# Dilation beside attention: half of a row's re-reading moved to the other of its two pieces

## The chip, the cores and the metric

The kernel runs on one core of a Trainium2 chip. The metric is the device time of one execution in microseconds (us), lower is better; the time of a kernel is the median of several executions.

## The reference

Sixteen graphs of 1024 nodes with 128 features pass through an attention layer and a graph layer of three rounds. What matters here is that both layers need the adjacency `adj` (16 x 1024 x 1024, f32): the attention masks and weights its scores with it, and the graph layer uses a *dilated* adjacency, from which entries were removed row by row in a fixed order, each removal seen by later rows:

```
# layer 0: attention over existing edges, weighted by adj
scores = einsum('bhnd,bhmd->bhnm', q, k) / sqrt(16)
scores = where(adj == 0, -inf, scores)
attn   = softmax(scores) * adj ;  attn /= attn.sum(-1) + 1e-8
# the pattern that layer 1 uses: n runs over the 1024 rows in order
row  = carry[n];  num = row.sum()
sf   = where(num > 10, (num + 1) // 2, 1)
rm   = row & (cumsum(row) % sf == 0)      # if num > 1 and the node is not masked
carry[n] = row & ~rm;  carry[:, n] &= ~rm # the column of the same node too
# layer 1: three rounds of  adj_dilated @ h / deg @ Wr + h @ Wx + b, normalised
```

## The kernel before, in words

**Attention.** For each graph `b`, column half `c` and 128-row block `m` of keys there is one turn (256 turns), and each turn has two *steps*, for `g` = 0 and 1, so that there are 512 steps. A step is: sixteen small matmuls that put minus infinity where there is no edge (line 554) and four score matmuls (560) on PE; two exponentials of 128x1024 on ACT (598); two products with the adjacency of 128x1024 on VectorE, DVE (603); and, one step later, eight value matmuls and eight sums on PE (487, 492). At `g` = 0 a turn also turns a block of `adj` over for the turn after next: load (188), transposes (505), ACT's copy and edge test (508, 512), the store of the turned block (509) and six small DMAs that copy the edge test to other partitions (516, 517; tile `nomask`). All DMAs named here are issued by SP, one after the other.

**Dilation.** It runs as a generator beside the attention, in eight blocks of 128 rows of all sixteen graphs (`k` = 0 to 7). In a block the removals inside the diagonal square are found by rounds of counting, and then each graph's row block is finished ("a row" below means one graph's 128 rows of the block, so a block has sixteen). The generator yields its cost and where its next piece may go; `beside_attention` (951) spends pieces at an even pace over the 512 steps, and a piece marked "A" comes only behind a step of `g` = 0, one marked "B" behind a step of `g` = 1, "1" behind either. PE, ACT and DVE run their instructions in the order in which they are written down; SP's DMAs are put in order by the framework's own scheduler.

**A row's two pieces** (the loop at 896, counter `i`, three rows in flight):
- the "A" piece: a running sum along row `i` on DVE (900, tile `both`), eight transposes of row `i - 2` on PE (907) and ACT's copy of them (909, tile `et`);
- the "B" piece: two absolute values for row `i` on ACT (915, `wr`); for row `i - 1` on DVE the removals (924, 928, 930, tile `er`); the fetch of an earlier block's removals for row `i + 1` (893, `gm`); and for row `b = i - 2` the re-reading for the next block: `read` takes the signs of the freshly loaded rows `ad` in two parts, the columns up to and with the next diagonal square (699) and the rest (703), each with a count; then on DVE the merge of row and column (937), the stores of the removals (938, 940, 942; `mr_d`), `survive` for row `b - 2` (716: takes the removed entries out of the signs, with a count), `fetch_removed` for `b` (710, tile `gl`) and the load of `ad` for row `i` (683).

The tiles `ad`, `gl`, `gm` and `et` have two buffers each. The last two calls of `survive` of a block, for rows 14 and 15, are made by `last_two` (721) between the first parts of the next block: one behind the product 749 and 750, one behind the first scan (756). The sixteenth row's `gl` is fetched from what the sixteenth row's `et` has just stored.

Of the kernel before, what the change touches and what calls it, by code (L numbers as in the profile page):

```python
# [15 lines left out]
AF = mybir.ActivationFunctionType  # L16
# [18 lines left out]
def swept(ctx: ExitStack, tc: tile.TileContext, t: dict, out: bass.AP, flag: bass.AP):  # L35
# [8 lines left out]
    nc = tc.nc  # L44
    x, adj, nodemask = t["x"], t["adj"], t["nodemask"]
    B, N, D = x.shape
# [120 lines left out]
    def first_part(p1):  # L167
# [90 lines left out]
        signs = one.tile([P, NB, 2, B], F32, name="signs")  # L258
# [200 lines left out]
        def fetch_first(b, queue):  # L459

            first_rows[b] = shared.tile([P, N], F32, name=f"ad_0_{b}", tag="mr", bufs=4)
            queue.dma_start(first_rows[b], adj[b, :P, :])
# [188 lines left out]
        def dilation():  # L651
# [9 lines left out]
            def rk(b, lo, hi):  # L661
                return rks[b // (B // 2)][:, b % (B // 2), lo:hi]

            blocks = {}
# [10 lines left out]
            def fetch(k, b):  # L675

                if k == 0:
                    if b not in first_rows:
                        fetch_first(b, nc.gpsimd)
                    blocks[0][2][b] = first_rows.pop(b)  # L680
                    return
                ad = shared.tile([P, N], F32, name=f"ad_{k}_{b}", tag="ad", bufs=2)
                nc.sync.dma_start(ad, adj[b, k * P : (k + 1) * P, :])
                blocks[k][2][b] = ad

            def read(k, b):
                ad = blocks[k][2].pop(b)
                n1 = (k + 1) * P
                if k == 0 and b % 2:
                    for part, of, count in (  # L690
                        (rk(b, 2, 2 + n1), ad[:, :n1], signs[:, k, 0, b : b + 1]),
                        (rk(b, 2 + n1, N + 2), ad[:, n1:], blocks[k][1][:, b : b + 1]),
                    ):
                        nc.vector.scalar_tensor_tensor(
                            part, of, 0.0, nothing.to_broadcast([P, of.shape[-1]]), ALU.add, ALU.not_equal,
                            accum_out=count,
                        )
                    return
                nc.scalar.activation(
                    rk(b, 2, 2 + n1), ad[:, :n1], AF.Sign, accum_out=signs[:, k, 0, b : b + 1]  # L700
                )
                if n1 < N:
                    nc.scalar.activation(
                        rk(b, 2 + n1, N + 2), ad[:, n1:], AF.Sign, accum_out=blocks[k][1][:, b : b + 1]
                    )

            def fetch_removed(k, b):
                if k > 0:
                    gl = shared.tile([P, N], BF, name=f"gl_{k}_{b}", tag="gl", bufs=2)
                    nc.sync.dma_start(gl[:, : k * P], mr_d[b][:, k, : k * P])  # L710
                    blocks[k][3][b] = gl

            def survive(k, b):
                if k > 0:
                    part = rk(b, 2, 2 + k * P)
                    nc.vector.scalar_tensor_tensor(
                        part, part, 0.0, blocks[k][3].pop(b)[:, : k * P], ALU.add, ALU.is_gt,
                        accum_out=blocks[k][0][:, b : b + 1],
                    )

            def last_two(k):
                for b in (B - 2, B - 1):
                    survive(k, b)
                    yield
# [11 lines left out]
            for k in range(NB):  # L736
                n0 = k * P
                n1 = n0 + P
# [62 lines left out]
                parts = small.tile([P, 2, B], F32, name=f"parts_{k}", tag="parts", bufs=2)  # L801
# [82 lines left out]
                more = k + 1 < NB  # L884
# [4 lines left out]
                def known(b):  # L889

                    if k > 0 and b < B:
                        gms[b] = shared.tile([P, N], BF, name=f"gm_{k}_{b}", tag="gm", bufs=2)
                        nc.sync.dma_start(gms[b][:, :n0], mr_d[b][:, k, :n0])

                known(0)
                for i in range(B + 2):
                    b = i
                    if b < B:
                        row = rk(b, 0, N + 2)
                        nc.vector.tensor_tensor_scan(  # L900
                            pair_sums[b % 2], row[:, 0::2], row[:, 1::2], 0.0, ALU.add, ALU.add
                        )
                    b = i - 2
                    if 0 <= b:
                        pe = ps_d.tile([P, NB, P], BF, name=f"pe_{k}_{b}", tag="d")
                        for j in range(NB):
                            nc.tensor.transpose(pe[:, j, :], ers[b][:, j * P : (j + 1) * P], ident_bf)
                        ets[b] = pool.tile([P, NB, P], BF, name=f"et_{k}_{b}", tag="et", bufs=2)
                        nc.scalar.copy(ets[b], pe)
                    yield (1.3 if i < B else 0.0), "B"  # L910
                    b = i
                    if b < B:
                        wrs[b] = pool.tile([P, N], F16, name=f"wr_{k}_{b}", tag="wr", bufs=2)
                        for t, at in enumerate((at_even, at_odd)):
                            nc.scalar.activation(  # L915
                                wrs[b][:, t * HN : (t + 1) * HN], pair_sums[b % 2][:, t : t + HN], AF.Abs,
                                bias=at[:, b : b + 1], scale=2.0,
                            )
                    b = i - 1
                    if 0 <= b < B:  # L920
                        er = ers[b] = pool.tile([P, N], BF, name=f"er_{k}_{b}", tag="er", bufs=3)
                        wr = wrs.pop(b)
                        for t in range(2):
                            nc.vector.tensor_scalar(
                                er[:, t::2], wr[:, t * HN : (t + 1) * HN], off[:, b : b + 1], allof[:, b : b + 1],
                                ALU.is_equal, ALU.max,
                            )
                        nc.vector.tensor_tensor(er, er, rk(b, 2, N + 2), ALU.mult)
                        if k > 0:
                            nc.vector.tensor_tensor(er[:, :n0], er[:, :n0], gms.pop(b)[:, :n0], ALU.max)  # L930
                    known(i + 1)
                    b = i - 2
                    if 0 <= b:
                        if more:
                            read(k + 1, b)
                        er, et = ers.pop(b), ets.pop(b)
                        nc.vector.tensor_tensor(er[:, n0:n1], er[:, n0:n1], et[:, k, :], ALU.max)
                        nc.sync.dma_start(mr_d[b][:, k, :n1], er[:, :n1])
                        if k > 0:
                            nc.sync.dma_start(mr_d[b][:, :k, n0:n1], et[:, :k, :])  # L940
                        if more:
                            nc.sync.dma_start(mr_d[b][:, k + 1 :, n0:n1], et[:, k + 1 :, :])
                            if b >= 2:
                                survive(k + 1, b - 2)
                            fetch_removed(k + 1, b)
                    if more and i < B:
                        fetch(k + 1, i)
                    yield (2.9 if i < B else 1.2), ("A" if i < B + 1 else 1)
                late = last_two(k + 1) if more else iter(())

        def beside_attention():
# [102 lines left out]
    def output_part(L, b, c, hT, prev, tag):  # L1054

        py = bank(f"py_{L}_{b}_{c}", tag).rearrange("p (k d) -> p k d", d=D)
        for i in range(HB):
            n = (c * HB + i) * P
            nc.tensor.matmul(py[:, i, :], hT[:, n : n + P], wts[f"Wl{L}"], start=True, stop=True)
        yield  # L1060
        k0 = c * HB
        for i in range(HB):
            k = k0 + i
            nc.vector.scalar_tensor_tensor(
                prev[:, k, :], py[:, i, :], mf2[:, b * NB + k : b * NB + k + 1], prev[:, k, :],
                ALU.mult, ALU.add,
            )
        if c == 1:
            nc.gpsimd.dma_start(acc_d[L][b], prev)
# [142 lines left out]
    with tc.manual_schedule(  # L1212
# [6 lines left out]
        for L in range(3):  # L1219
# [10 lines left out]
            for b in range(B):  # L1230
                more = b + 1 < B
# [3 lines left out]
                for c in range(2):  # L1235
                    i = (L * B + b) * 2 + c
# [10 lines left out]
                    parts = []  # L1247
                    if c == 1 and L > 0:
                        at_end = b + 2 >= B
                        parts = [output_part(L - 1, b, h, hT, prev, held.pop(0) if at_end else "y") for h in range(2)]  # L1250
# [727 lines left out]
```

## Time and profile before

| | |
|---|---|
| three runs | 3395.78, 3398.22 and 3401.01 us, median 3398.22 |
| the profiled execution | 3396.91 us, of which the span from the first to the last instruction is 3395.1 |
| granted TensorE clock | 0.995 |
| the attention's exponentials | first at 20.1 us, last step at 2318.0: 4.50 us a step |
| of it, one row of a block (two steps) | 9.2 us in blocks 0 to 3, 9.7 in block 6, 8.9 in block 7 |
| signs, first part (699), 128x256 to 128x1024 | 425 ns to 1054 ns |
| signs, second part (703), 128x768 to 128x128 | 848 ns to 308 ns |
| `survive` (716), 128x128 to 128x896 | 284 ns to 1083 ns, and 82 ns to read its count |
| `gl` (710), issue to landing | 1.6 to 6.2 us, median 3.6 |
| `nomask` (516, 517), issue to landing | median 2.7 us |

A step is timed from the start of its first exponential to that of the next step's. Engines: PE is TensorE, DVE VectorE, ACT ScalarE, POOL GpSimd, SP the engine that issues DMAs. A group of instructions is read as: line, engine, operation, output<-inputs, shape, count | busy us, mean ns of one | idle time of the engine just before them and what ended it. The profiled execution is one run; sums below are made against its own time.

### The profile page before, as it was taken

How to read it: one execution, taken by the hardware profiler on the slowest of the kernel's cores; microseconds unless marked ns; L12 is line 12 of the kernel's file. 1: busy time of each engine (PE TensorE's matmuls, PEld its weight loads, DVE VectorE, ACT ScalarE, POOL GpSimd, SP SyncE). 2: the span in 40 equal slices, each digit the busy share in tenths (PEclk: the TensorE clock that was granted, in tenths of full speed). 3: DMA queues.
4: the chain of work that ended last, by engine and by line, in shares of the span. 5: the costliest groups of instructions: out<-in, count | busy, mean ns of one | idle time of the engine just before them, and what ended most of it. 6: DMA issues, size and time to landing. Idle time of an engine off the chain costs nothing. (4 is left out here: it accounts for less than half of the span.)

```text
span 3395.1 us, 86338 instructions
## 1 busy us (share of the span) xinstructions
PE 3310.6 (98%) x34855; PEld 1872.4 (55%) x34855; DVE 3025.5 (89%) x5399; ACT 2305.4 (68%) x3909; POOL 164.2 (5%) x253
## 2 busy tenths in 40 slices
PE   8999999999999999999999999999999899999997
PEld 3333333333333333333334334336999899999997
DVE  7898989989989998998998999897888899988887
ACT  7699689779879969968976986884232344423334
POOL 2000000000000000000000000000000000000000
PEclk9999999999999999999999999999999999999999
DMA  7357456547637736845863773677999799989996
GB/s 242 108 168 206 137 149 199 161 129 221 188 122 213 221 122 183 238 144 158 236 190 122 237 240 119 189 228 261 346 341 343 284 353 350 353 323 350 352 351 222
DMA packets 650123, 772.28 MB, mean 227 GB/s; under 512 B 173264, under 2 KB 569168, under 8 KB 637424
## 3 DMA queue, kind: packets, MB, share of 16 engines
q1 hardware_dynamic: 632672, 708.58, 64.4%
q0 software_dynamic: 15456, 57.30, 5.0%
q8 instruction: 275, 4.51, 0.6%
q14 instruction: 136, 1.11, 0.1%
q10 hardware_dynamic: 1584, 0.79, 0.1%
HBM read 508.50 MB, written 157.29 MB: 196 GB/s over the span
## 5 line engine op out<-in xcount | busy, mean ns | idle before, releaser
L603 DVE TENSOR_TENSOR w<-e,aT 128x1024 f32<-128x1024 f32 x1024 | 1205.5, 1219 | 138.4 <-ACT e L598 136.8
L598 ACT ACTIVATE e<-sc 128x1024 f32<-128x1024 f32 x1024 | 991.9, 1022 | 333.6 <-PE sc L560 332.6
L1132 PE MATMUL pg<-y,aT 128*128 128x128 f32 (+1 forms) x6144 | 729.8, 275 | 0.0
L1132 PEld LDWEIGHTS pg<-y,aT 128*128 128x128 f32 x6144 | 707.9, 192 | 0.0
L487 PE MATMUL acc<-w,both 128*32 128x512 f32 x4096 | 586.7, 605 | 3.1 <-DVE w L603 2.6
L560 PE MATMUL sc<-qT,kT 32*128 32x512 f32 x4096 | 584.4, 640 | 0.3 <-ACT qT L315 0.3
L492 PE MATMUL acc<-e,eps 128*32 128x512 f32 x4096 | 573.1, 592 | 0.0
L146 DVE SCALAR_TENSOR_TENSOR aT<-mr,aT 128x1024 f32<-128x1024 bf16 x384 | 458.8, 1217 | 0.0
L492 PEld LDWEIGHTS acc<-e,eps 128*32 128x32 f32 x4096 | 150.6, 110 | 294.6 <-issue 289.6
L1155 ACT ACTIVATE sq<-o 128x512 f32<-128x512 f32 x96 | 60.6, 631 | 328.5 <-DVE o L1150 328.5
L554 PEld LDWEIGHTS <-never 32*32 32x32 bf16 x8192 | 80.9, 88 | 347.9 <-issue 325.6
L554 PE MATMUL sc<-nomask,never 32*32 32x512 bf16 x8192 | 252.3, 385 | 16.8 <-ACT e L598 12.3
L1173 ACT COPY hT<-pt 128x512 f32<-128x512 f32 x96 | 56.3, 586 | 289.3 <-PE pt L1169 280.0
L560 PEld LDWEIGHTS sc<-qT,kT 32*128 32x128 f32 x4096 | 160.1, 183 | 116.9 <-issue 116.1
L505 PEld LDWEIGHTS pa<-ident,a 128*128 128x128 f32 x1024 | 107.7, 141 | 181.4 <-issue 129.7
L487 PEld LDWEIGHTS acc<-w,both 128*32 128x32 f32 x4096 | 92.8, 108 | 156.2 <-issue 65.4
L915 ACT ACTIVATE wr<-both,th 128x512 f16<-128x512 f16 x256 | 172.1, 730 | 7.1 <-DVE both L900 6.9
L505 PE MATMUL pa<-ident,a 128*128 128x128 f32 x1024 | 168.3, 287 | 6.4 <-DMA a<-in_adj 5.7
L512 ACT ACTIVATE nomask<-aT 128x512 bf16<-128x512 f32 x256 | 161.4, 630 | 8.1
L1150 DVE SCALAR_TENSOR_TENSOR o<-pg,rdeg,mine 128x128 f32<-128x128 f32 x384 | 108.1, 344 | 55.9 <-PE pg L1132 52.6
L508 ACT COPY aT<-pa 128x512 f32<-128x512 f32 x256 | 152.7, 597 | 5.3 <-PE pa L505 4.3
L900 DVE TENSOR_TENSOR_SCAN both<-rk 128x513 f16<-128x513 bf16 x128 | 155.9, 1218 | 0.0
(228 smaller groups left out, 3894.9 us busy)
## 6 DMA issues: line engine op xcount, KB each, us to landing
aT<-aT_d SPq DMA_DIRECT2D x94, 2048.0 KB, 9.9
mr<-mr_d SPq DMA_DIRECT2D x188, 512.0 KB, 6.0
aT_d<-aT SPq DMA_DIRECT2D x256, 256.0 KB, 4.0
a<-in_adj SPq DMA_DIRECT2D x253, 256.0 KB, 3.7
ad<-in_adj SPq DMA_DIRECT2D x112, 512.0 KB, 4.2
nomask<-nomask SPq DMA_DIRECT2D x512, 96.0 KB, 2.7
nomask<-nomask SPq DMA_DIRECT2D x512, 64.0 KB, 2.7
nomask<-nomask SPq DMA_DIRECT2D x512, 32.0 KB, 2.7
```

Source lines behind the costliest of these rows:

```text
L146: nc.vector.scalar_tensor_tensor(part, mrs[h][:, j : j + 2, :].rearrange("p j n -> p (j n)"), 0.0, part, ALU.is_equal, ALU.mult)
L487: nc.tensor.matmul(acc[g][32 * j : 32 * j + 32, :], v1[:, m, (2 * j + g) * HW : (2 * j + g) * HW + 32], ws[j // 2][:, j % 2, :], start=(m ...
L492: nc.tensor.matmul(acc[g][32 * j : 32 * j + 32, :], eps8, es[j // 2][:, j % 2, :], start=False, stop=(m == NB - 1),)
L505: nc.tensor.transpose(pa[:, k * P : (k + 1) * P], a[:, k, :], ident)
L512: nc.scalar.activation(nomask[:, 0, :], aT[:, 0, :], AF.Relu, bias=1.0, scale=-1e38, accum_out=zeros[:, i : i + 1])
L554: nc.tensor.matmul(scs[j // 2][to : to + 32, j % 2, :], never[rows, rows], nomask[rows, j, :], start=True, stop=False, tile_position=(32 * ...
L560: nc.tensor.matmul(scs[j // 2][:, j % 2, :], kT[rows, mm], qTs[c][rows, g, :], start=False, stop=True, tile_position=(32 * j, 0),)
L598: nc.scalar.activation(e, scs[q], AF.Exp, scale=1.0 / math.sqrt(HD))
L603: nc.vector.tensor_tensor(w, es[q], aT.to_broadcast([P, 2, HN]), ALU.mult)
L900: nc.vector.tensor_tensor_scan(pair_sums[b % 2], row[:, 0::2], row[:, 1::2], 0.0, ALU.add, ALU.add)
L915: nc.scalar.activation(wrs[b][:, t * HN : (t + 1) * HN], pair_sums[b % 2][:, t : t + HN], AF.Abs, bias=at[:, b : b + 1], scale=2.0,)
L1132: nc.tensor.matmul(pg[:, i // 2, at : at + width], aT[:, j, i * P : (i + 1) * P], y[:, j, :width], start=(j == 0), stop=(j == NB - 1),)
```

## The change

In each row's piece, the second part of the signs (703), `survive`, `fetch_removed` and the load of the next `ad` leave the "B" piece and are put at the front of the "A" piece that follows it, half a row later; for row 15 they come in the first piece of the next block. The costs that pieces are given change so that each row's sum stays as it was (1.3 + 2.9 becomes 2.1 + 2.1). No instruction is added or taken away.

```diff
-            def read(k, b):
-                ad = blocks[k][2].pop(b)
+            def read(k, b, parts=(0, 1)):
+                ad = blocks[k][2][b] if parts == (0,) else blocks[k][2].pop(b)
...
-                nc.scalar.activation(
-                    rk(b, 2, 2 + n1), ad[:, :n1], AF.Sign, accum_out=signs[:, k, 0, b : b + 1]
-                )
-                if n1 < N:
+                if 0 in parts:
+                    nc.scalar.activation(
+                        rk(b, 2, 2 + n1), ad[:, :n1], AF.Sign, accum_out=signs[:, k, 0, b : b + 1]
+                    )
+                if 1 in parts and n1 < N:
...
+                def other_half(b):
+                    if more and b >= 0:
+                        read(k + 1, b, (1,))
+                        if b >= 2:
+                            survive(k + 1, b - 2)
+                        fetch_removed(k + 1, b)
+                    if more and 0 <= b + 2 < B:
+                        fetch(k + 1, b + 2)
+
                 known(0)
                 for i in range(B + 2):
+                    other_half(i - 3)
...
-                    yield (1.3 if i < B else 0.0), "B"
+                    yield (2.1 if i < B else 0.8), "B"
...
-                            read(k + 1, b)
+                            read(k + 1, b, (0,))
...
-                            if b >= 2:
-                                survive(k + 1, b - 2)
-                            fetch_removed(k + 1, b)
-                    if more and i < B:
-                        fetch(k + 1, i)
-                    yield (2.9 if i < B else 1.2), ("A" if i < B + 1 else 1)
+                    yield (2.1 if i < B else 0.4), ("A" if i < B + 1 else 1)
+                other_half(B - 1)
                 late = last_two(k + 1) if more else iter(())
```

The program that results has every other piece at the same step as before. On SP, in block 4's last row as an example, the order before was: `et` stores, `er` store (938), `gl`, `ad`, `a` (188), `aT_d` (509), six `nomask`. After it is: `et` stores, `ad`, `er` store, `a`, `aT_d`, six `nomask`, `gl`, `ad`. It is the same in blocks 0, 1, 2, 5 and 6 (without the `ad` loads in block 6); in block 3 `gl` stands right behind `a`.

## The prediction

> **What bounds the kernel now.** I read the page's busy shares first, then busy time in thirteen rows (i = 3 to 15) of each block, then SP's waits, then the timeline where one block ends and the next begins.
>
> ```profile
> span 3395.1 us, 86338 instructions
> ...
> PE 3310.6 (98%) x34855; PEld 1872.4 (55%) x34855; DVE 3025.5 (89%) x5399; ACT 2305.4 (68%) x3909; POOL 164.2 (5%) x253
> ...
> L716 DVE SCALAR_TENSOR_TENSOR rk<-rk,gl 128x768 bf16<-128x768 bf16 x16 | 15.2, 952 | 1.2 <-DMA gl<-mr_d 1.2
> ```
>
> No engine is the bound by its share alone; ACT's 68% is an average over unlike stages. The last line is to be kept in mind: of 112 calls of `survive`, DVE waits for a `gl` 1.2 us before one of the sixteen in block 5 (0.8 and 0.3 in blocks 1 and 3). The windows below are the rows of blocks 0, 2, 4, 5, 6 and 7: length; busy PE, weight loads, DVE, ACT, POOL; clock; DMA.
>
> ```profile
> 196.80:316.30 119.50, 116.60 (x1266) 43.30 (x1262) 106.52 (x171) 118.74 (x210) 2.81 (x3) 1.00 0.69 198
> ...
> 751.30:870.90 119.60, 116.04 (x1263) 43.65 (x1259) 114.25 (x185) 118.36 (x209) 3.88 (x6) 1.00 0.74 214
> ...
> 1306.20:1427.80 121.60, 117.59 (x1260) 44.43 (x1259) 119.15 (x198) 119.59 (x211) 5.00 (x6) 1.00 0.79 235
> 1587.50:1711.00 123.50, 118.69 (x1253) 45.17 (x1246) 120.10 (x196) 119.92 (x212) 5.00 (x6) 1.00 0.81 239
> 1872.40:1998.80 126.40, 120.89 (x1260) 44.53 (x1263) 123.38 (x197) 119.99 (x188) 4.97 (x6) 1.00 0.81 244
> 2157.90:2273.40 115.50, 112.96 (x1250) 41.14 (x1251) 110.00 (x156) 102.62 (x149) 6.60 (x10) 1.00 0.75 226
> ```
>
> Inside the rows ACT is busy 99% of the time in blocks 0 to 3; DVE draws level in block 4 and passes it in 5 and 6. Block 7, without signs, runs shorter. Cut at each step's start, ACT works 4.1 us in "A" and 5.1 in "B"; DVE, cut at its own line 603, 3.8 in "A" and 4.45 (block 0) to 5.75 (block 6) in "B". The halves are uneven, but their buffers join them: in blocks 0 to 3 ACT stands idle only about 0.1 us a row.
>
> Where a block ends, the picture is another. Timeline, last row of block 4:
>
> ```profile
> 1450.15 0.47 SPq L938 DMA_DIRECT2D mr_d<-er  x1
> ...
> 1451.64 0.33 SPq L710 DMA_DIRECT2D gl<-mr_d  x1
> 1452.07 0.38 SPq L683 DMA_DIRECT2D ad<-in_adj  x1
> 1452.54 0.38 SPq L188 DMA_DIRECT2D a<-in_adj  x1
> 1452.93 2.28 DVE L756 TENSOR_TENSOR_SCAN w<-go_on,up 128x1024 f16<-128x1024 bf16 x1
> ...
> 1455.13 0.80 DVE L716 SCALAR_TENSOR_TENSOR rk<-rk,gl 128x640 bf16<-128x640 bf16 x1
> ...
> 1455.86 2.35 DVE L603 TENSOR_TENSOR w<-e,aT 128x1024 f32<-128x1024 f32 x2
> ...
> 1457.70 0.59 SPq L517 DMA_DIRECT2D nomask<-nomask  x1
> ```
>
> `gl` of row 15 leaves SP at 1451.64 and lands at 1454.42; the last `survive` reads it at 1455.13, with attention's products right behind it on DVE. So 0.7 us are to spare. From 1445.2 to 1472.4 DVE is busy 26.14 of 27.2 us, ACT 18.55: here DVE leads.
>
> **The change part by part.**
>
> *Second signs, "B" to "A".* ACT's sum per row is unchanged. The part costs 848 ns (block 0, for block 1's row), 741, 634, 527, 418, 308 and nothing (block 6): ACT becomes about 4.95/4.25 in block 0, 4.5/4.8 in block 5, unchanged in block 6. Its price is bounded above by nothing removed, and below by all idle time being recovered: window less the busier of ACT and DVE, over blocks 0 to 6, is 0.8 + 0.9 + 1.2 + 1.5 + 2.0 + 3.4 + 3.0 = 12.8 us (blocks 1 and 3 read the same way). A loss would need ACT to wait for scores; they are made 1.5 us after an exponential ends, and at least 2 us of other ACT work stays between exponentials in either half.
>
> *survive, "B" to "A", 0.28 to 1.08 us and 0.08 for its count.* DVE becomes 4.1/4.1 in block 0 and 4.9/4.7 in block 6. Queued behind it in "A" are the running sum and then "B"'s products. ACT's 915 waits for that sum, 1.56 us after it in block 0 and 0.58 in block 6 on average. But in "B" the same instruction no longer stands before the "A" products, which now start 0.11 (block 0) to 1.72 us (block 6) after their exponentials: what is put in front of the sum is mostly given back there. I price both moves inside the rows together at -4 us of the possible 12.8, nearer to nothing because blocks 0 to 3 have no idle time to give, and keep -12.8 and +5 (0.05 us a row in 112 rows, half the ACT idle seen) as ends.
>
> *The new costs* of the pieces shift nothing: every other piece keeps its step. *The load of `ad`* comes half a row later; it is read about 14 us later at a landing of 4.2 (median). Hidden; uncovered it would cost ACT at most that 4.2 a row.
>
> *fetch_removed.* Inside the rows a `gl` has some 10 us between landing and its `survive`, and both move by half a row: nothing. It also gains: before, SP stood waiting for the store of `et` to land:
>
> ```profile
> SPq L710 <- DMA mr_d<-et: 70.4, 66, 3.4
> ```
>
> That wait is 1.1 us each of 66 times and goes, as eight other DMAs are now in between. At a block's end, though, the two readers in `last_two` do not move: `survive` of row 15 still stands behind the first scan, while `gl` of row 15 is now issued behind `a`, `aT_d` and the six `nomask` (the order on SP in the section on the change). Those take 5.3 us on SP in block 0 (338.83 to 344.14) and 5.75 in block 4 (1452.54 to 1458.29). Counted from the `er` store's issue: before, `gl` follows after 1.5 to 1.9 us; after, after 0.5 + 0.9 + the six `nomask` (3.75 to 4.8). From the difference I take 0.6 (row 14's landing wait, 1.1, is gone earlier; an `ad` of 0.5 has come in; 1.1 in block 6, which has no such `ad`).
>
> | block | `gl` landed | later by | `survive` started | DVE late by |
> |---|---|---|---|---|
> | 0 | 341.87 | 3.45 | 342.51 | 2.8 |
> | 1 | 620.88 | 2.6 | 620.90 | 2.6 |
> | 2 | 897.9 (issue + 3.1, the median of the others) | 2.85 | 898.90 | 1.9 |
> | 3 | `gl` stands behind `a` alone | 0 | 1176.87 | 0 |
> | 4 | 1454.42 | 4.0 | 1455.13 | 3.3 |
> | 5 | 1740.08 | 4.1 | 1740.10 | 4.1 |
> | 6 | 2025.05 | 2.5 | 2026.05 | 1.5 |
>
> The sum is 16.2 us. Who waits behind it: DVE's products of the next step, PE's value matmuls of them, then scores and exponentials. How much passes through? In block 4 the value matmuls begin at 1458.40, 1.3 us after the first product is done; but DVE runs on without a gap to 1470, and at 1463.3 and 1468.5 PE is already waiting for it (0.32 and 0.72 us). A late DVE therefore stays late: I take all 16. The lower bound takes off that 1.3 at six ends, leaving 8; the upper one adds row 14's `gl`, which moves too (in blocks 1, 3 and 5 by my count 2 us past its reader), and is 24.
>
> *Order of `nomask`.* It comes about 1.5 us earlier at a block's end. Once this helps: in block 1 PE's mask matmuls at 616.64 wait for a `nomask`. -1 us.
>
> [...]
>
> **The sum**: -4 - 1 + 16 = +11 us on the profiled execution's 3396.9 (3395.1 of span and 1.8 around it): 3408. That execution lay 1.3 below the runs' median, so I forecast 3409 against 3398.2.
>
> **The rivals.**
>
> *Balance wins, faster.* If `gl` of row 15 lands in time after all (its place on SP matters only if SP is behind; it decides when SP reaches the last `nomask` less than 1 us after the old issue of `gl`), only the moves in the rows count: -5 to -13, about 3390. For it: DVE and ACT both stand idle 0.2 to 0.5 us a row in blocks 5 and 6. Against: SP issued the store of row 15's `er` 4.5 to 8.0 us after DVE had it ready (937), in all seven blocks, so SP is behind. Chance 0.13.
>
> *The late DVE is absorbed, no change.* Inside the rows a product is ready 0.9 to 2.1 us before its matmul; if that spring is there at the ends too, 8 us pass, 4 come back and 1: +3, 3401. Against it stand the two PE waits above. Chance 0.22.
>
> *SP chokes in the rows too, slower still.* `gl` now waits for a `survive` of the same piece, and everything on SP behind it, the next `nomask` too, waits as well. `nomask` lands 3 to 6 us before its matmuls on average; if that is used up, 0.2 us a row in 112 rows, 22 more: 3430. Against: SP gets to `gl` some 7 us into the piece, DVE to `survive` at 4. Chance 0.08.
>
> **How the numbers follow.** The forecast has 0.57, with its own range 3402 to 3418. A difference under 0.2% (6.8 us) can't be told from none here, so slower begins at 3405.0 and faster ends at 3391.4. Slower: 0.08, and 0.52 of the forecast's 0.57: 0.60. Same: 0.22 and 0.05 of the forecast, 0.27. Faster: 0.13. The range, 3393 to 3424, leaves out most of the fast case and the choke.
>
> **What would show it.** Right: six idle times of DVE before 716, ended by `gl`, of 1.5 to 4 us, none in block 3; the steps at a block's end longer by as much; windows inside the rows shorter by up to 0.3 us a row in blocks 5 and 6; ACT's busy time unchanged. Wrong: `gl` landing before its `survive` everywhere; or those waits there and the next block's first removals no later; or rows longer, with PE waiting for `nomask`.

## The result, and the profile after

| | before | after |
|---|---|---|
| median | 3396.41 us (3393.52 to 3401.01, 6 runs) | 3427.61 us (3419.55 to 3432.16, 6 runs) |
| ratio to before | | 1.0087, 95% interval 1.0072 to 1.0102 |
| profiled execution, its span | 3396.91, 3395.1 us | 3428.24, 3426.4 us |
| attention's last step begins at | 2318.0 us | 2346.9 us |

The change made the kernel 31 us slower; 11 were forecast, with 3424 as the upper end. 28.9 of the 31.3 us between the two spans are lost inside attention, and 2.4 behind it, where executions of the same code differ by as much (see "What stays open"). Cut at the steps of the exponentials, they lie so (a row of a block is two steps; lines of the changed kernel behind 698 are 1 to 11 higher than before: `survive` is 717, the fetch of `gl` 711, the first signs 700, the second 704):

| part, all blocks together | after less before, us |
|---|---|
| rows 0 to 2 | -3.4 |
| rows 3 to 15 | +4.2 |
| block ends: the ten steps behind the rows, blocks 0 to 6 | +29.5: 0.8, 2.8, 4.7, 1.0, 6.1, 7.1, 7.0 |
| ahead of the rows of block 0 | -1.2 |
| the rest between the blocks | -0.2 |

The first line is no gain: one second reading of signs (848 ns in block 0 to 308 in block 5) has left that stretch for the block's end, where the same time comes back. So the ends lose about 26 and the rows 4.

The page of after, its span and the busy time of each engine:

```profile
span 3426.4 us, 86274 instructions
...
PE 3317.4 (97%) x34855; PEld 1864.2 (54%) x34855; DVE 3026.4 (88%) x5399; ACT 2304.6 (67%) x3909; POOL 161.5 (5%) x253
```

The busy time of DVE and ACT is the same as before to 1 us: to these two nothing was added but waiting. PE's grew by 6.8 us. The waits of after name it (engine, tile and line that waited <- what it waited for: us in all, times, longest):

```profile
ACT e L598 <- PE sc L560: 343.2, 266, 9.9
...
PEld acc L487 <- DVE w L603: 63.6, 103, 5.6
...
DVE rk L717 <- DMA gl<-mr_d: 18.9, 8, 4.9
...
ACT rk L700 <- DMA ad<-in_adj: 15.6, 16, 2.0
```

The same four before:

```profile
ACT e L598 <- PE sc L560: 332.6, 284, 4.0
...
PEld acc L487 <- DVE w L603: 47.0, 99, 1.5
...
DVE rk L716 <- DMA gl<-mr_d: 2.3, 3, 1.2
...
ACT rk L699 <- DMA ad<-in_adj: 1.9, 2, 1.3
```

Of the last two, the wait for `gl` was forecast, and the one for `ad` was said to be hidden. The longest wait of ACT for scores (first line) has grown from 4.0 to 9.9 us, and PE's weight loads wait 63.6 us for products where it was 47.0. The windows of rows 3 to 15 in blocks 0, 2, 4, 5, 6 and 7 (length; busy PE, weight loads, DVE, ACT, POOL; clock; DMA):

```profile
194.77:313.99 119.22, 116.49 (x1264) 42.66 (x1262) 106.63 (x170) 118.66 (x209) 3.02 (x3) 1.00 0.71 200
751.50:873.10 121.60, 117.40 (x1271) 42.66 (x1267) 114.31 (x183) 118.42 (x211) 3.94 (x6) 1.00 0.73 211
1315.73:1437.40 121.67, 116.67 (x1262) 42.65 (x1261) 118.86 (x197) 119.70 (x212) 4.65 (x6) 1.00 0.79 227
1602.69:1726.36 123.67, 117.50 (x1257) 43.08 (x1250) 120.21 (x196) 120.00 (x212) 4.79 (x6) 1.00 0.79 233
1894.82:2021.16 126.34, 119.88 (x1266) 42.81 (x1270) 123.33 (x197) 119.92 (x188) 4.89 (x6) 1.00 0.83 237
2187.38:2302.27 114.89, 112.39 (x1250) 41.02 (x1251) 109.99 (x156) 102.53 (x148) 6.58 (x10) 1.00 0.76 228
```

Blocks 4, 5 and 6 last as long as before (121.60, 123.50, 126.40): balanced halves brought nothing. Block 2 is 2.0 us longer than its 119.60, with ACT still busy 118.42: 3.2 us of idle time in place of 1.2. Timeline of three places: the row of block 2 in which ACT waits, the end of block 4 on SP, and what follows it on DVE, PE and ACT (start, us, engine, line, operation; in brackets the idle time before it and what ended it):

```profile
848.69 0.53 SPq L711 DMA_DIRECT2D gl<-mr_d  x1
...
849.32 0.38 SPq L683 DMA_DIRECT2D ad<-in_adj  x1
...
853.50 0.63 ACT L700 ACTIVATE rk<-ad 128x512 bf16<-128x512 f32 x1 [1.56 <-DMA ad<-in_adj]
...
1468.32 0.33 SPq L711 DMA_DIRECT2D gl<-mr_d  x1
...
1470.60 0.83 DVE L717 SCALAR_TENSOR_TENSOR rk<-rk,gl 128x640 bf16<-128x640 bf16 x1 [3.09 <-DMA gl<-mr_d]
...
1471.35 2.36 DVE L603 TENSOR_TENSOR w<-e,aT 128x1024 f32<-128x1024 f32 x2
...
1472.62 2.08 PE L487 MATMUL acc<-w,both 128*32 128x512 f32 x6 [2.63 <-DVE w L603]
...
1474.48 1.08 PE L487 MATMUL acc<-w,both 128*32 128x512 f32 x2
...
1474.51 2.76 PE L492 MATMUL acc<-e,eps 128*32 128x512 f32 x6
...
1479.34 1.02 ACT L598 ACTIVATE e<-sc 128x1024 f32<-128x1024 f32 x1 [7.90 <-PE sc L560]
```

In block 2 `ad` is issued 4.2 us before ACT reads it, and its landing takes 4.2. At block 4's end `gl` leaves SP at 1468.32, and the chain runs down the lines: DVE waits 3.09 us, its product is late, PE stands 2.63 us for it, then PE itself is slow (2.76 us for the last six matmuls, where six of line 492 took 1.27 at 1466.00), and ACT waits 7.90 us for the scores behind them. The windows of that stretch show why:

```profile
1437.40:1488.12 50.72, 47.47 (x477) 16.10 (x476) 42.49 (x67) 34.92 (x59) 0.00 (x0) 0.97 0.67 196
1474.00:1477.20 3.20, 3.20 (x12) 0.39 (x5) 3.20 (x5) 0.00 (x0) 0.00 (x0) 0.50 0.33 98
```

The granted TensorE clock is 0.50 in the 3.2 us that follow the wait. Such stretches came behind PE's idle time at five block ends: 3.41 us long in blocks 1, 2, 4 and 6, 6.83 us in block 5. Before, the clock was 1.00 from 19 us to the end of attention.

### The profile page after: what moved, and what is told of

Its sections match the earlier page's. It is cut to its first block, busy times and chain, and to the rows that moved or that the text cites. A ratio compares the mean times of both kernels' runs of the same rounds, so it can differ in the third digit from the quotient of the medians.

```text
span 3426.4 us, 86274 instructions
## 1 busy us (share of the span) xinstructions
PE 3317.4 (97%) x34855; PEld 1864.2 (54%) x34855; DVE 3026.4 (88%) x5399; ACT 2304.6 (67%) x3909; POOL 161.5 (5%) x253
## 5 line engine op out<-in xcount | busy, mean ns | idle before, releaser
L487 PEld LDWEIGHTS acc<-w,both 128*32 128x32 f32 x4096 | 89.2, 108 | 172.9 <-DVE w L603 63.6
```

The costliest lines, as they stand in the source:

```text
L487: nc.tensor.matmul(acc[g][32 * j : 32 * j + 32, :], v1[:, m, (2 * j + g) * HW : (2 * j + g) * HW + 32], ws[j // 2][:, j % 2, :], start=(m ...
```

## The experiments

Twelve kernels, each timed in turn with the kernel before. "Waits" are of the profiled execution: DVE for `gl` before `survive`, ACT for `ad` before the first signs. "Rows" and "ends" are rows 3 to 15 and the block ends, against before; the last column counts the times that the granted clock fell to 0.5 inside the blocks.

| run | median us | ratio to before (95%) | wait `gl` | wait `ad` | rows | ends | clock |
|---|---|---|---|---|---|---|---|
| after | 3427.61 | 1.0087 (1.0072 to 1.0102) | 18.9 | 15.6 | +4.2 | +29.5 | 5 |
| e1 ends undone | 3415.93 | 1.0056 (1.0041 to 1.0070) | 13.3 | 20.0 | +8.7 | +14.8 | 0 |
| e2 late `gl` only | 3423.37 | 1.0077 (1.0064 to 1.0090) | 23.9 | 1.8 | -0.8 | +26.8 | 4 |
| e3 readers later | 3408.57 | 1.0024 (1.0013 to 1.0035) | 2.4 | 22.5 | +11.0 | +8.3 | 0 |
| e5 PE kept busy | 3425.12 | 1.0079 (1.0066 to 1.0092) | 18.0 | 17.0 | +7.9 | +23.8 | 0 |
| e7 signs and load only | 3541.34 | 1.0420 (1.0404 to 1.0437) | 16.8 | 137.0 | +101.3 | +44.0 | 6 |
| e11 removal only | 3415.54 | 1.0063 (1.0048 to 1.0078) | 19.6 | 2.1 | -0.1 | +21.8 | 3 |
| e8 load split | 3455.07 | 1.0178 (1.0164 to 1.0192) | 30.9 | 1.5 | +15.0 | +40.8 | 5 |
| e10 before, readers later | 3393.29 | 0.9993 (0.9984 to 1.0002) | none | 1.9 | +0.5 | -0.1 | 0 |
| f1 `gl` on POOL | 3399.11 | 1.0000 (0.9991 to 1.0009) | 1.5 | 2.9 | +2.6 | +3.8 | 1 |
| f2 `ad` on POOL | 3419.53 | 1.0060 (1.0046 to 1.0074) | 17.2 | 4.3 | +0.8 | +24.3 | 3 |
| f3 both on POOL | 3399.26 | 1.0000 (0.9991 to 1.0009) | 4.8 | 4.6 | +1.4 | +8.7 | 1 |
| f4 before, `gl` on POOL | 3397.48 | 0.9999 (0.9990 to 1.0008) | 2.9 | 2.4 | -0.2 | -1.0 | 0 |

**Where is the loss: ends or rows?** e1 puts `survive` and `fetch_removed` of rows 14 and 15 back into piece "A":

```diff
     read(k + 1, b, (1,))
-    if b >= 2:
-        survive(k + 1, b - 2)
-    fetch_removed(k + 1, b)
+    if b < B - 2:
+        if b >= 2:
+            survive(k + 1, b - 2)
+        fetch_removed(k + 1, b)
...
     nc.sync.dma_start(mr_d[b][:, k + 1 :, n0:n1], et[:, k + 1 :, :])
+    if b >= B - 2:
+        survive(k + 1, b - 2)
+        fetch_removed(k + 1, b)
```

> The changed kernel, but for rows 14 and 15 of each block survive and fetch_removed go back to where they were: in piece "A", behind the stores of the row. Second signs, the load of ad and rows 0 to 13 stay as changed. Theory 1 (the loss sits at the block ends: 19.0 us of DVE waits for a late gl before line 717, and half-rate TensorE clock behind them): the block ends give back about 29 of the 31 us, so about 3398 us (3392 to 3404), no DVE wait over 1.3 us before the survive of row 15, no granted clock of 0.5 between 30 and 2300 us. Rival 2 (the loss is spread over the rows: SP filled by 14 transfers a row, survive in front of the running sum, the loads of ad read late): those are all still there, so over 3415.

It came back only by 12 us, and DVE still waits for `gl` of row 15 at six ends (0.2 to 3.5 us). Timeline of its block 4:

```profile
1466.19 0.52 SPq L683 DMA_DIRECT2D ad<-in_adj  x1
1466.81 0.38 SPq L950 DMA_DIRECT2D mr_d<-er  x1
1467.84 0.32 SPq L711 DMA_DIRECT2D gl<-mr_d  x1
...
1473.29 0.82 DVE L717 SCALAR_TENSOR_TENSOR rk<-rk,gl 128x640 bf16<-128x640 bf16 x1 [3.45 <-DMA gl<-mr_d]
```

`gl` stands behind the `er` store again, but a load of `ad` (512 KB) is now issued right ahead of both; before, it followed them. This `gl` took 5.42 us to land, against 2.78 before, and counted from the end of row 15 it was also issued 3.1 us later (26.9 against 23.8). So neither theory holds as it was put: `gl` can be late without the eight places on SP, too. That the `ad` in front of it stretched its landing was not tested by itself. e2 does to the kernel before what e1 undid:

```diff
+def fetch_later(b):
+    if more and b >= B - 2:
+        survive(k + 1, b - 2)
+        fetch_removed(k + 1, b)
...
 for i in range(B + 2):
+    fetch_later(i - 3)
```

> The kernel before, with one part of the change alone: survive and fetch_removed of rows 14 and 15 of each block stand half a row later, as in the changed kernel; everything else is as before. Theory 1: this alone costs nearly the whole loss: 3396 + 25 to 31 = 3421 to 3428, with DVE waits for gl before the survive of row 15 that sum to 14 to 20 us, and a granted clock of 0.5 for 3.4 us behind the longer ones. Rival 2 (loss in the rows): within 4 us of the kernel before. Rival 3 (the wait costs its own length and the clock nothing): 3396 + 16 to 19 = 3412 to 3415.

This alone costs 27 us of the 31, all of it at the ends, as theory 1 said; rival 3's 16 to 19 is too little, as the waits themselves sum to 23.9 here. What rival 3 says of the clock is not refuted by that: 21.6 of the 26.8 us at the ends are new waits.

**Is it the late reader or the transfers' place?** e3 leaves out the first of the two calls of `last_two`:

```diff
 nc.vector.tensor_scalar(up[:, :, 0:1], up[:, :, 0:1], 1024.0, None, ALU.add)
-next(late, None)
 yield 1.3, 1
```

> The changed kernel with one line left out: the first of the two places that call last_two. The survive of row 14 then stands behind the first scan and that of row 15 behind the second, one step (some 5 us) later each; the fetches stay late. Theory 1 (gl comes 2 to 5 us too late for its reader, and all follows from it): the waits before line 717 are gone or under 0.5 us, no clock of 0.5 in attention, about 3398 us (3392 to 3404). Rival 4 (the place of the transfers on SP hurts by itself, as they hold up the nomask copies behind them or the stores): the loss stays, over 3415.

The clock stretches at the ends go, as expected, and the waits for `gl` nearly so (2.4 us are left, 1.9 of them in block 6), but the time stops at 3408.6, over theory 1's 3404: what is left are mainly ACT's waits for `ad`, 22.5 us, and rows 11 us longer. (Its profiled execution, 3416, was the longest of its seven.)

**What does the clock cost?** e5 keeps PE busy while DVE waits:

```diff
 for hb in halves:
+    if hb.start and k in (2, 3, 5, 6, 7):
+        beat = ps_d.tile([P, 512], F32, name=f"beat_{k}", tag="d")
+        for _ in range(11):
+            nc.tensor.matmul(
+                beat, upto, go_on[:, 0:4, :].rearrange("p b i -> p (b i)"), start=True, stop=True
+            )
     nc.vector.tensor_tensor_scan(
```

> The changed kernel, with 11 matmuls 128x512 in bf16 (about 0.21 us each at the granted clock of 1.0, 2.3 us together, into a PSUM tile that nobody reads) put on PE ahead of the scores of the step in which DVE waits for gl of row 15, at the ends of blocks 1, 2, 4, 5 and 6. The DVE waits stay. Theory 1 (of the 29.5 us at the block ends about 19 are the waits, and about 10 the half-rate clock of 3.41 us, four times, and 6.83 us, once, that follows PE's idle time): PE's idle time before the value matmuls falls from 2.0, 3.8, 2.6, 4.8, 2.7 to about 0, 1.5, 0.3, 2.5, 0.3 us, the half-rate stretches go at three or more of the five ends, and the time falls by 5 to 9 us from 3427.6, to 3418 to 3423, though PE does 11 us more work. Rival 3 (the clock costs nothing, as PE is waiting for DVE there anyway): no half-rate stretches and still 3426 to 3430, or a few us above.

Timeline of its block 4:

```profile
1470.51 2.55 PE L760 MATMUL beat<-go_on,upto 128*128 128x512 bf16 x11
1474.25 0.82 DVE L717 SCALAR_TENSOR_TENSOR rk<-rk,gl 128x640 bf16<-128x640 bf16 x1 [3.50 <-DMA gl<-mr_d]
...
1476.27 1.76 PE L487 MATMUL acc<-w,both 128*32 128x512 f32 x6 [0.49 <-DVE w L603]
```

DVE waits about as long as in after, PE only 0.49 us, and the clock stays at 1.00 in all of attention. At the five ends with a wait, the steps grew by 20.8 us in e5 and 27.7 in after, with DVE waits of 17.3 and 19.0 us (rows 14 and 15 of these blocks). What exceeds the waits is 3.5 and 8.7 us (2.0 of each the second signs that moved there), so by this pair the half-rate clock is worth about 5 us, at the lower edge of what was expected. Two other readings do not bear this out. The medians are only 2.5 us apart, their intervals overlap, and e5's 3425.1 lies between theory 1's range and rival 3's. And e2, with half-rate stretches at four of the same five ends and no signs moved there, grew by 25.1 us at them with waits of 22.8: 2.2 us above its waits, where e5, with no such stretch, has 1.5 besides the signs. So the price lies between nothing and about 5 us, and these runs do not settle it.

**The two halves of the change.** e7 and e11 each make one half alone:

```diff
 read(k + 1, b, (1,))
-if b >= 2:
-    survive(k + 1, b - 2)
-fetch_removed(k + 1, b)
...
 nc.sync.dma_start(mr_d[b][:, k + 1 :, n0:n1], et[:, k + 1 :, :])
+if b >= 2:
+    survive(k + 1, b - 2)
+fetch_removed(k + 1, b)
```

> One half of the change alone: second signs and the load of ad half a row later, as in the changed kernel, while survive and fetch_removed stand in piece "A" as before, for all rows. Theory 5 (two losses that do not add up: the load of ad, half a row later, now lands after ACT wants to read it, and at the block ends it is issued on SP straight ahead of the gl of row 15, whose landing grows from 1.9 to 4.0 us before to 3.5 to 5.4): ACT waits for ad of 0.3 to 3 us in blocks 1 to 3, rows 3 to 15 longer by 6 to 11 us in all, gl of row 15 waited for at some ends, together 3410 to 3418. Theory 6 (the halves balanced are a gain, and the load is hidden): 3388 to 3396. Theory 7 (neither does anything): 3394 to 3402.

e11 starts from the kernel before; its `fetch_later` is e2's without the condition on rows 14 and 15.

> The other half alone: survive and fetch_removed of all rows half a row later, as in the changed kernel, second signs and the load of ad as before. Theory 5 (the late gl at the block ends is the whole loss of this half; in the rows a survive in front of the running sum costs nothing): as the late gl of the last two rows alone, 3419 to 3428, and rows 3 to 15 unchanged within 2 us in all. Rival 2 (survive in front of the running sum, or more of SP's time, costs in each row): 3430 or more, with the rows 5 us longer or more. If both halves simply added, this one and the one with signs and load would sum to more than the changed kernel's +31.

They don't add: +145 and +19 us, and +31 together. e11 was some 4 us better than expected (SP's waits for the store of `et` are 27.4 us there, before 70.4, and the ends of blocks 0 to 3 lose nothing). e7 was far off every theory. Timeline of a row of its block 2, SP alone:

```profile
805.59 0.53 SPq L683 DMA_DIRECT2D ad<-in_adj  x1
806.22 0.38 SPq L948 DMA_DIRECT2D mr_d<-et  x1
806.65 0.46 SPq L950 DMA_DIRECT2D mr_d<-et  x1
810.53 0.33 SPq L711 DMA_DIRECT2D gl<-mr_d  x1
810.95 0.38 SPq L894 DMA_DIRECT2D gm<-mr_d  x1
811.43 0.38 SPq L946 DMA_DIRECT2D mr_d<-er  x1
```

and its waits:

```profile
SPq L711 <- DMA mr_d<-et: 246.9, 108, 4.3
```

```profile
ACT rk L700 <- DMA ad<-in_adj: 137.0, 71, 4.8
```

`gl` may only be issued once the store of `et` has landed. Before, `ad`, `gm` and the `er` store filled that landing; with `ad` gone to the front, SP stands 3.4 us at `gl` in this row, and everything behind it is late, the next `ad` first. The late fetch of `gl` is thus what makes the late load of `ad` bearable at all.

**Is `ad` late by its half row, or by SP?** e8 cuts the load in two, each part behind the signs that free its place:

```diff
-nc.sync.dma_start(ad, adj[b, k * P : (k + 1) * P, :])
+if 0 in parts:
+    nc.sync.dma_start(ad[:, :n1], adj[b, k * P : (k + 1) * P, :n1])
+if 1 in parts and n1 < N:
+    nc.sync.dma_start(ad[:, n1:], adj[b, k * P : (k + 1) * P, n1:])
...
-    if more and 0 <= b + 2 < B:
-        fetch(k + 1, b + 2)
+    if more and 2 <= b + 2 < B:
+        fetch(k + 1, b + 2, (1,))
...
+    if more and i < B:
+        fetch(k + 1, i, (0, 1) if i < 2 else (0,))
     yield (2.1 if i < B else 0.4), ("A" if i < B + 1 else 1)
```

> The changed kernel, with the load of ad of rows 2 to 15 cut in two: the columns of the first part are fetched into their place right behind the first signs of the row that held it, as early as before, the other columns behind the second signs. One transfer more a row on SP. Theory 5 (ACT's waits for ad come from the half row that the load lost): the waits of ACT for ad in blocks 1 to 3 go, the rows 3 to 15 give back the 4 to 11 us that they lost, the late gl at the ends stays, about 3417 to 3424. Rival 2 (SP full): the transfer more, some 0.4 us on SP in each of 98 rows, makes it slower than the changed kernel, over 3432.

Both were right in part: ACT's waits for `ad` fall from 15.6 to 1.5 us, and yet the kernel is 27 us slower than after. One transfer more a row makes SP late for the others: `gl` is waited for 30.9 us, and PE's mask matmuls wait for `nomask`, 8.7 us against 1.4 in after. In rows 3 to 15 of block 2 SP issues 13.8 transfers a row before, 13.7 in after and 14.5 in e8, and they fill 81, 81 and 82% of its time, its waits the better part of the rest. That SP's time is the scarce thing is what these numbers suggest. f1 to f3 test it by taking transfers from SP, with `nc.gpsimd` in place of `nc.sync` for one load or both:

```diff
-nc.sync.dma_start(gl[:, : k * P], mr_d[b][:, k, : k * P])
+nc.gpsimd.dma_start(gl[:, : k * P], mr_d[b][:, k, : k * P])
...
-nc.sync.dma_start(ad, adj[b, k * P : (k + 1) * P, :])
+nc.gpsimd.dma_start(ad, adj[b, k * P : (k + 1) * P, :])
```

> The changed kernel, with fetch_removed's load of gl issued by GpSimd (POOL) in place of SP. It then stands behind no nomask, a or aT_d, and SP has one transfer less a row and no wait for the store of et to land (55.6 us in the changed kernel). Theory 5 (the place on SP makes gl of rows 14 and 15 late, and SP's lag makes ad late): the DVE waits before line 717 fall from 19 us to under 4, no half-rate clock in attention, ACT's waits for ad fall from 15.6 us to under 6: 3396 to 3406. Rival 8 (it is the landing, not the place): the landing stays 2 to 4 us and gl late, 3415 or more. If only the ad part stays: 3404 to 3412.

> The changed kernel, with the load of ad issued by GpSimd in place of SP; gl stays on SP. Theory 5: ACT's waits for ad fall from 15.6 us to under 5 and rows 3 to 15 of blocks 1 to 3 lose what they had grown by (4 to 11 us); with one transfer less a row SP also comes earlier to the gl at the block ends, whose waits shrink by some 0.5 us each but stay: 3412 to 3422. Rival 9 (ad is late because its buffer comes free late, wherever it is issued): ACT's waits for ad stay over 10 us, and the time within 5 us of 3427.

> The changed kernel, with both loads, gl and ad, issued by GpSimd. Theory 5: neither is late any more, SP has two transfers less a row; what is left is the balance of the halves alone: 3390 to 3400, at best 6 us under the kernel before (the -4 that the prediction gave the balance). If gl stands behind an ad that waits for its buffer on GpSimd's queue, gl is late again: over 3410.

f1, with `gl` alone moved, takes back 28.5 us and stands at the kernel before, within 0.1%. Its waits:

```profile
POOL gl L711 <- DMA mr_d<-et: 573.4, 41, 59.8
POOL gl L711 <- DVE rk L717: 425.2, 53, 12.9
...
ACT rk L700 <- DMA ad<-in_adj: 2.9, 5, 1.1
...
DVE rk L717 <- DMA gl<-mr_d: 1.5, 1, 1.5
```

The waiting that `gl` does (for the store of `et`, and for `survive` to free its buffer) has not gone; it stands on an engine where almost nothing is behind it (POOL is busy 224.9 us in f1, 7% of the span). `ad`, still on SP and still half a row late, is in time as well, so its lateness too was SP's more than its own. f2 cures `ad` (4.3 us) and leaves `gl` (17.2), and the time follows `gl`: 3419.5. SP has a transfer less a row in f2 as it has in f1, but `gl` keeps its place there, so it is the place and not the number of transfers that makes `gl` late. f3 has both loads moved and is no better than f1; its 3399.3 is the upper edge of theory 5's 3390 to 3400, and the balance is worth nothing that can be measured.

**A version that beats both?** e10 is the kernel before with e3's edit, f4 the kernel before with f1's:

> The kernel before, with the first of the two places that call last_two left out, so that survive of rows 14 and 15 stand one step later behind the first and the second scan. Theory 1: the 1.2, 0.8 and 0.3 us of waits for gl at the ends of blocks 5, 1 and 3 go: 0 to 3 us faster than before, 3393 to 3399. Rival: the later survive falls into a step in which DVE is busier: 1 to 6 us slower.

> The kernel before, with the load of gl issued by GpSimd. SP loses its 70 us of waits for the store of et and one transfer a row. As no engine of attention waits for SP in the rows before (1.2 us of waits for nomask, 2.3 for gl), theory 5 expects little: 3390 to 3397. Rival: DVE and GpSimd get in each other's way, and the time rises by 5 us or more.

Neither can be told from the kernel before (0.9993 and 0.9999, both intervals hold 1). Nothing tried here beats it.

## Why the prediction was wrong

*Where the miss lies.* Against the forecast's +11 the two spans differ by 31.3 us, 20 more. The block ends, forecast at +16 and -1, cost 26: 11 of the 20. The rows, forecast at -4, cost 4: 8 more. 2.4 came behind attention, and 1.4 were gained elsewhere. The steps that failed are the size of the term of +16, the word "hidden" for the load of `ad`, and the -4.

*The sign and the place were right.* `gl` of row 15 is late for an unmoved `survive` because it has slipped behind `a`, `aT_d` and six `nomask` on SP: e2 (+27 with this alone), f1 (0 with its place on SP taken away) and f2 (its place kept, 17.2 us of waits) show it.

*The term of +16 was too small, and its sum of waits is near by luck.* The waits before `survive` of row 15 came to 0, 2.18, 3.64, 0, 3.09, 4.88 and 2.64 us where 2.8, 2.6, 1.9, 0, 3.3, 4.1 and 1.5 were forecast: 16.4 against 16.2, the sum near, the single blocks not, and 2.3 of the 16.4 had been there before. Block 0 escaped: counted from the end of row 15, `gl` was issued 2.3 us later than before where 3.45 were forecast, it landed 2.0 us after its issue in place of 3.45, and its reader came 0.8 us later. Row 14, which I kept for the upper bound only, brought 2.6 more, so that the new waits come to 16.7 us. And the sum ended at DVE, each microsecond of its waits counted as one of time: the ends cost 26. The 9 us on top are not waits for `gl`. I followed the wait to PE and did not ask what PE's idle time does to PE; the half-rate clock behind it is worth at most about 5 of them. But e5, where the clock stays at 1.00, also loses some 5 us more at the ends than its new waits, and what that is stays open. The table of windows carries that clock in every row, at 1.00; the forecast used it for the stages as they were, not for the stage with a new hole in it.

*"Hidden", said of the load of `ad`, is the step that failed in the rows.* "Read about 14 us later at a landing of 4.2" was the distance before the change (medians of 13.6 to 16.5 us in blocks 0 to 5). After, it is 5.5 to 8.2: part of it goes by the edit, and more because SP issues it 4 to 12 us after its buffer has come free, in place of 0 to 10 before. In f2, where POOL mostly issues it 0.4 us after that, 13 us are left: the half row alone would have stayed hidden. In some rows of blocks 1 to 3 nothing is left between landing and reading. The sentence had a price for the uncovered case, 4.2 a row, and the sum and the range took none of it. The rows lost 4.2 us in after's profiled execution and 8 to 11 in those of e1, e3 and e5, and nothing in e2 and e11, where the load and the second signs have their old place; in f2, with the signs moved and `ad` mostly in time, they lost 0.8. In the time, f2 has a ratio of 1.0060 where after has 1.0087, though SP has a transfer less there too.

*The -1 for `nomask` does not show in the time*: PE's mask matmuls wait for it 1.4 us in all, before 1.3 (their weight loads not at all, before 1.5).

*The -4 inside the rows is 0.* The windows of blocks 4 to 6 are as long as before, f1 and f3 stand at the time of before. I had seen that buffers join the halves and still took a third of a bound; DVE and ACT together fill these rows, and moving work between halves that buffers already join moved nothing.

*The rivals.* "Absorbed" fails: in sum the ends grew by no less than DVE's new waits. "Balance wins" fails with the -4. "SP chokes in the rows too" had the right engine and the wrong carrier: not `nomask` (1.4 us of waits in after) but `ad`; e8 shows that one transfer more is enough for `nomask` as well.

*What stays open.* How the 31 us split is known only to a few microseconds: about 17 new waits for `gl`, 9 more at the ends, of which the clock can be up to 5 and the rest is unexplained, and 4 in the rows, for the most part `ad`. Taken one at a time the parts don't add, which fits lags of one queue. The 2.4 us behind attention are not the change's: no kernel here differs there, and its length varies from 1074.3 to 1080.0 us over the fourteen profiled executions (before 1077.1, after 1079.5; e5, with the change, 1074.9). The clock was at 0.50 there for 30.9 us before and for 37.6 us in after; that this sets the length was not shown.

## What to carry to other kernels

When a transfer is moved, follow the issuing queue, not the transfer: what stands ahead of it now, what it was filling in (in e7, the landing that `gl` waits for), and how long after its buffer comes free the queue gets to it. A queue whose issues alone filled four fifths of the time (81% in block 2's rows) was a bound like an engine here (in e8 one transfer more a row cost 27 us), and a load that must wait for something belongs on a queue with nothing urgent behind it: here one word, sync to gpsimd, undid the whole loss (f1: 28.5 us, ratio 1.0000). And behind a new wait ahead of PE, look at the clock as well as at the wait (in after it was 0.50 for 3.41 us behind 2.02 us of idle time).

## What was not expected of the hardware

TensorE's granted clock fell to 0.50 after idle times of PE of only 2.02, 2.63 and 2.68 us (and 3.82 and 4.78) in after. Behind the shorter ones of its attention (1.49 us and less), and behind all in the attention of before (1.22 us and less), it stayed at 1.00. Their length is not all that counts: in e1 PE's longest wait for products was 2.1 us, and the clock did not fall at any end. What else counts was not shown.

What it takes to issue a DMA, with the waits that stand in the issuing queue, was worth 28.5 us here: that is what moving the 112 loads of `gl` from SP to GpSimd took back (after against f1).
